# Two residual blocks in one kernel: where norms, moves, products, banks and relus of the Gram stages stand

## The chip, the cores and the metric

The kernel runs on one core of one Trainium2 chip, in fp32. The metric is device time in microseconds (us), the median of several runs. Engines are named as in the profile: PE (TensorE, matrix products), PEld (its weight loads), DVE (VectorE), ACT (ScalarE), POOL (GpSimd) and SP (the sync engine, which issues DMA transfers).

## The reference

Two bottleneck blocks follow each other, with weights of their own, on x of 64 x 1024 x 14 x 14. The batch norms use the statistics of the batch itself, so each needs the whole of the convolution ahead of it before its scale and shift are known.

```python
def block(x, w1, b1, g1, be1, w2, b2, g2, be2, w3, b3, g3, be3, residual_scale):
    out = relu(bn(conv(x, w1, b1, 1, 0), g1, be1))      # 1x1, 1024 -> 256
    out = relu(bn(conv(out, w2, b2, 1, 1), g2, be2))    # 3x3, 256 -> 256
    out = bn(conv(out, w3, b3, 1, 0), g3, be3)          # 1x1, 256 -> 1024
    out = softplus(residual_scale)[0] * out
    return relu(x + out)
# bn: mean and variance over (batch, height, width), eps 1e-5
```

## The kernel before, in words

All images' pixels (12,544) of the 256 middle channels stay on chip in one tile, `y_all`, as two slots of 128 channels. The work goes in stages, for each layer b = 0 and 1: conv1 (for layer 1 interleaved with layer 0's last convolution, in `fused`), conv2 (`conv2`, a Winograd form), the Gram stage (`gram` and `conv3_stats`), and the last convolution with the residual (`residual`, then `fused` for layer 0, `final` for layer 1).

**Why there is a Gram stage.** The third batch norm needs mean and variance of conv3's output, which isn't kept. They follow from the sums and the 256 x 256 matrix of products (the Gram matrix) of y after its norm, less a centre: the mean square of output channel o is w_o^T G w_o, and its mean comes from the sums. So `gram` makes G on TensorE, and `conv3_stats` multiplies it with w3.

**The begin of `gram` (L997 to L1176).** A product over pixels needs the pixels on the partitions, so y has to be transposed, 256 pixels at a time (`px`, one "pair" of column blocks). 49 pairs come out of the generator `pairs` (L1109). Two ways of transposing are used:

- `by_tensor` (L1081): four TensorE transposes into a PSUM bank, and a DVE add of the centre (L1093) into a tile `zt`. The first 8 pairs go this way; their pixels are the pieces `still`, of 4 pairs each.
- `by_vector` (L1099): DVE transposes 32 x 32 blocks (L1102) of a copy, `home(k)`, in which DMAs have already put the blocks in place (`move`, L1058, 16 DMAs for the first two pieces, 12 and four ACT copies, `stay`, for the others). These are the pieces `moved`: the first of 5 pairs, then six of 6 pairs. In layer 0 the second home is the tile `ws`, otherwise homes are x tiles.

Before a piece can be moved it is normed (`normed`, ACT, with relu, one instruction for each slot) and its centre is subtracted (`less`, DVE, L1044). The kept pieces are normed only. ACT, DVE and TensorE work of this stage is pinned to the order of the source (`tc.keep_in_program_order`), and each engine works its queue in that order; the order is written by hand, as conditions on the number n of the pair just yielded. DMAs of a `move` go to SP or POOL by their number, which is a list in L1064. TensorE takes the products of pair k after the transposes of pair k + 1: eight products into the two banks `upper` ("cp") and `lower` ("ap") for each of its two column blocks.

**The end: `conv3_stats` (L1178).** Only a part of the symmetric G is computed, with weights once or twice 1/12544 in `by`. DVE scales the banks into g0 and g1 (`scaled`, L1185), TensorE multiplies with w3 (for each half of the output channels: t0 and t1, the left and right halves of g0 and g1's columns, L1210), DVE multiplies by w3 again and adds (L1213, L1214), and TensorE sums over partitions by products with ones (into "ax" and "ap"). One conv3 product of image pair 0 (`made`) stands ahead of all that. `affine` then makes scale and shift in a chain of small DVE instructions.

**`residual` (L1225)** handles the first image pair: for each of 8 output groups a product (those in `made` exist already), a DVE add with scale (L1233), an ACT relu with shift (L1234), and one DMA for the whole. Which PSUM bank a product takes is by tag: the tags given, or for the others the cycle in `Psum`. In layer 0 only two products are in `made`; in layer 1 six.

**`fused` (L1270)** starts with 14 steps (`LAG`) of the last convolutions alone. A step is one product; what follows a product (`after1` and so on: a copy `cu` on ACT, a DVE add) is issued at the next step. The order of a unit is p1, p2, p6, p5, p7; p6 adds into the bank that `cu` copies after p1, and p7 into the one copied after p6.

Of the kernel before, what the change touches and what calls it, by code (L numbers as in the profile page):

```python
# [88 lines left out]
def bottlenecks(ctx: ExitStack, tc: tile.TileContext, x, w1s, w2s, w3s, pars, out):  # L89
# [907 lines left out]
    def gram(psum, pool, homes, aff, minus_c, beside):  # L997
# [60 lines left out]
        def move(k):  # L1058
            x, a, run = home(k)
            for i, j in itertools.product(range(4), range(4)):  # L1060
                if k > 1 and i == j:
                    continue
                n = 4 * i + j if k < 2 else 3 * i + j - (j > i)
                queue = nc.gpsimd if n in ((1, 3, 6, 8, 10, 13, 15) if k < 2 else (1, 3, 6, 8, 10)) else nc.sync  # L1064
                ins = queue.dma_start(  # L1065
                    out=x[32 * i : 32 * i + 32, :, j], in_=y_all[32 * j : 32 * j + 32, :, a + i * run : a + i * run + run]
                )
                tc.keep_in_program_order(ins)
# [40 lines left out]
        def pairs():  # L1109

            for a in 0, px:
                norm_vector(1, y_all[:, 1, a : a + px], aff)
                normed(a, a + px, (0,))
            center_row()
            normed(2 * px, 4 * px)
            rest = [(piece, s) for piece in still for s in range(MS)]
            for n, a in enumerate(a for piece in still for a in range(*piece, px)):
                yield by_tensor(a)
                if n == 0:
                    busy(psum, "ax", 1)  # L1120
                    normed(*moved[0])
                elif n == 1:
                    less(*moved[0])
                    move(0)
                    normed(*still[1])
                elif n == 3:
                    normed(*moved[1])
                elif n == 4:
                    less(*moved[1], both[:1])
                    normed(*moved[2])  # L1130
                elif n == 5:
                    less(*moved[1], both[1:])
                    move(1)
                elif n == 6:
                    less(*moved[2], both[:1])
                    normed(*moved[3])
            for k, (a, e) in enumerate(moved):
                for i in range((e - a) // px):
                    yield by_vector(k, i)
                    if k == 0 and i == 1:  # L1140
                        less(*moved[2], both[1:])
                        move(2)
                        stay(2)
                    elif i in (1, 3) and k and k + 2 < len(moved):
                        less(*moved[k + 2], both[i // 2 : i // 2 + 1])
                        if i == 3:
                            move(k + 2)
                            if k + 3 < len(moved):
                                normed(*moved[k + 3])
                            stay(k + 2)  # L1150
                    elif i in (0, 5) and k > 1 and rest:
                        piece, s = rest.pop(0)
                        less(*piece, (s,))
            assert not rest
# [23 lines left out]
    def conv3_stats(psum, one, grams, w3, mv, tags, spare):  # L1178
# [7 lines left out]

        scaled(g0[low], 0, upper[low], by[0][low])
        scaled(g0[high], Q + 1, upper[high], by[0][high])
        scaled(g1[low], 2 * Q + 1, lower[low, : 2 * Q + 1], by[1][low])
        n = Q + 1  # L1190
        for a, k in (1, 0), (3 * Q + 1, 1):
            scaled(g1[high], a, lower[high, k * n : k * n + n], by[1][high, k * n : k * n + n])
# [12 lines left out]
        for h in range(2):  # L1205
            cols = slice(h * half, (h + 1) * half)
            t0, t1 = (psum.tile(half * P, tag) for tag in tags[2 * h : 2 * h + 2])
            for i, g in enumerate((g0, g1)):
                for n, t in enumerate((t0, t1)):
                    matmul(t, g[:, 1 + n * P : 1 + n * P + P], w3[:, i, cols, :], start=i == 0, stop=i == 1)  # L1210
            qs = [q[:, s, h * half * P : (h + 1) * half * P] for s in range(MS)]
            for s, t in ((0, t0), (1, t1)):
                nc.vector.tensor_mul(qs[s], t, w3[:, s, cols, :].rearrange("p o c -> p (o c)"))  # L1213
            nc.vector.tensor_add(qs[0], qs[0], qs[1])  # L1214
# [10 lines left out]
    def residual(psum, xt, b, t, w3, aff, made=()):  # L1225
# [4 lines left out]
        for o in range(CS):  # L1230
# [3 lines left out]
            nc.scalar.activation(v, v, AF.Relu, bias=shift[:, o : o + 1])  # L1234

            step = CS if not tail else 1 if o + 2 >= CS else 2
            if (o + 1) % step == 0:
                queue = nc.gpsimd if step == CS else nc.scalar if o + 1 == CS else nc.sync
                queue.dma_start(
                    out=to[:, (o + 1 - step) * PX : (o + 1) * PX],  # L1240
                    in_=xt[:, o + 1 - step : o + 1, :].rearrange("p s f -> p (s f)"),
                )

# [26 lines left out]
    def fused(psum, pool, xpool, xs, w1, w3, aff, par, stats, one_done):  # L1270
# [18 lines left out]
        for i in range(LAG):  # L1289
            next(c)  # L1290
        while True:
# [164 lines left out]
    for b in range(2):  # L1456
# [7 lines left out]
        with tc.tile_pool(name=f"last_{b}", bufs=1) as one, tc.tile_pool(  # L1464
# [6 lines left out]
            with ExitStack() as scope:  # L1471
# [22 lines left out]
                if b == 1:  # L1494
                    made += [conv3(psum, 0, o, w3, tag) for o, tag in zip(range(2, 6), ("cy", "cp") * 2)]
# [4 lines left out]
                residual(psum, xs[0], b, 0, w3, aff, made)  # L1500
                weights = made_a + made_c
                with tc.tile_pool(name=f"rest_{b}", bufs=1) as pool:
# [5 lines left out]
                    fused(psum, pool, xpool, xs, *weights, aff, par[b + 1], stats1, one_done)  # L1508
# [40 lines left out]
```

## Time and profile before

| | us |
|---|---|
| median of 3 runs | 1932.78 (1932.09 to 1934.12) |
| the profiled execution, own time | 1934.62 |
| its span, first to last instruction | 1932.8 |
| PE busy, share of span | 1907.8, 99% |
| DVE busy | 1545.2, 80% |
| ACT busy | 1080.9, 56% |
| POOL busy | 563.8, 29% |
| Gram stage of layer 0, first to last `zt` product | 589.8 to 651.8 |
| Gram stage of layer 1, first to last `zt` product | 1550.0 to 1613.6 |

The profile is of one execution. "Busy" counts the time in which at least one instruction of an engine ran. A line of waits gives the waiting engine, the tile and source line of the waiting instruction, the one that released it, and then the sum, the number and the longest of these waits. A line of windows gives a stretch of time, the busy time of each engine with its number of instructions, the granted clock of TensorE as a share of full speed, the share of the DMA engines' time that was used, and GB/s. A line of the timeline gives start, duration, engine, source line, operation, written and read tiles, shape and count; a bracket at the end gives the idle time ahead of it and what ended it. A line of the chain gives start, duration and what the chain of work that ended last ran through.

### The profile page before, as it was taken

To read this page: it belongs to the slowest core of one execution; us is meant where nothing else is said; L and a number is where in the kernel's file an instruction comes from. 1 tells how busy PE (TensorE), PEld (TensorE's weight loads), DVE (VectorE), ACT (ScalarE), POOL (GpSimd) and SP (SyncE) were. 2 spreads that over 40 slices of the span, in tenths; PEclk is the share of its full clock that TensorE was granted. 3 is DMA by queue.
4 is the path that set the end of the run, shared out by engine and by line. 5 is a ranking of instruction groups with operands and counts; after the bars stand their busy time and mean duration, and the time that the engine had idled before them with its cause. 6 is when DMAs were issued, how large, how long until landed. Compare 5 with 4: busy or idle time off the path is not lost.

```text
span 1932.8 us, 28746 instructions
## 1 busy us (share of the span) xinstructions
PE 1907.8 (99%) x10246; PEld 1602.5 (83%) x10246; DVE 1545.2 (80%) x2481; ACT 1080.9 (56%) x2142; POOL 563.8 (29%) x680
## 2 busy tenths in 40 slices
PE   9999999999999999999999999999999999999999
PEld 5555557999997799999999999989999977555555
DVE  5778767999997767676776767689999986888886
ACT  2222214677777255555555555556777682666666
POOL 0111100211204133333433334302121041666664
PEclk9999999999999999999999999999999999999999
DMA  7777634787946534444444444258788466899998
GB/s 290 276 244 271 229 136 156 198 221 208 226 153 178 183 150 184 168 167 171 180 183 167 167 174 179 115 179 211 215 206 225 131 175 228 289 326 337 338 339 302
DMA packets 199071, 409.56 MB, mean 212 GB/s; under 512 B 37168, under 2 KB 175536, under 8 KB 182416
## 3 DMA queue, kind: packets, MB, share of 16 engines
q1 hardware_dynamic: 160128, 322.40, 48.4%
q0 software_dynamic: 33184, 34.25, 8.6%
q10 hardware_dynamic: 5616, 51.06, 6.3%
q8 instruction: 81, 1.33, 0.3%
q14 instruction: 62, 0.51, 0.1%
HBM read 263.75 MB, written 115.34 MB: 196 GB/s over the span
## 4 chain that ended last, share of the span: by engine, by line
PE 93%; DVE 3%; DMA 1%; ACT 1%; issue 1%; SPq 0%; POOL 0%; DVEq 0%; ACTq 0%; POOLq 0%
PE cy L171 17%; PE ay L171 17%; PE columns L171 13%; PE cp L171 12%; PE ap L171 10%; PE m L171 7%; PE l L171 6%; PE cx L171 5%; PE ax L171 4%; PE ps L171 1%; ACT y L334 0%; DMA home<-y 0%; DMA x<-mid 0%; SPq L1065 0%; DMA ws<-y 0%
## 5 line engine op out<-in xcount | busy, mean ns | idle before, releaser
L334 ACT ACTIVATE cu<-cy,scale 128x196 f32<-128x196 f32 (+1 forms) x552 | 256.8, 474 | 276.9 <-PE cy L171 271.7
L171 PE MATMUL columns<-v,ub 128*128 128x224 f32 (+1 forms) x1536 | 300.7, 337 | 0.0
L334 ACT ACTIVATE x<-x,shift 128x392 f32<-128x392 f32 x428 | 241.0, 613 | 59.6 <-POOL x L493 53.1
L171 PEld LDWEIGHTS columns<-v,ub 128*128 128x128 f32 x1536 | 269.2, 188 | 2.8
L467 DVE SCALAR_TENSOR_TENSOR x<-cp,scale,x 128x196 f32<-128x196 f32 (+1 forms) x368 | 178.0, 484 | 97.8 <-PE cp L171 96.5
L171 PE MATMUL cy<-ct,ws 128*128 128x196 f32 (+1 forms) x736 | 221.9, 383 | 1.8 <-ACT cu L334 1.7
L488 POOL TENSOR_TENSOR x<-x,cu 128x196 f32<-128x196 f32 (+1 forms) x184 | 159.7, 868 | 172.9 <-ACT cu L334 165.0
L171 PE MATMUL ay<-at,ws 128*128 128x196 f32 (+1 forms) x752 | 209.1, 381 | 0.0
L493 POOL TENSOR_TENSOR x<-x,cu 128x392 f32<-128x392 f32 x124 | 125.8, 1014 | 191.5 <-DVE x L467 191.5
L171 PEld LDWEIGHTS ay<-at,ws 128*128 128x128 f32 x752 | 136.5, 190 | 33.4
L171 PEld LDWEIGHTS cy<-ct,ws 128*128 128x128 f32 x736 | 133.4, 190 | 37.0 <-ACT cu L334 5.3
L171 PE MATMUL l<-diffs,ub 128*128 128x224 f32 (+1 forms) x768 | 149.1, 337 | 2.6 <-PE columns L171 2.6
L514 POOL TENSOR_TENSOR x<-x,cu 128x392 f32<-128x392 f32 x120 | 122.0, 1017 | 86.2 <-DVE x L467 71.8
L171 PE MATMUL m<-sums,ua 128*128 128x224 f32 (+1 forms) x752 | 145.9, 337 | 1.1 <-DVE sums L625 1.1
L334 ACT ACTIVATE au<-ay 128x196 f32<-128x196 f32 (+1 forms) x141 | 53.8, 381 | 156.9 <-PE ay L171 152.1
L171 PEld LDWEIGHTS l<-diffs,ub 128*128 128x128 f32 x768 | 134.3, 189 | 4.4 <-PE columns L171 3.9
L467 DVE SCALAR_TENSOR_TENSOR x<-cx,scale,x 128x196 f32<-128x196 f32 (+1 forms) x184 | 89.0, 484 | 57.0 <-PE cx L171 56.8
L171 PEld LDWEIGHTS m<-sums,ua 128*128 128x128 f32 x752 | 131.3, 189 | 2.9 <-DVE sums L625 2.5
L171 PE MATMUL cy<-y,w 128*128 128x196 f32 (+1 forms) x408 | 125.3, 393 | 0.0
L171 PE MATMUL cx<-y,w 128*128 128x196 f32 (+1 forms) x400 | 122.7, 391 | 0.0
L171 PE MATMUL cp<-y,ws 128*128 128x196 f32 (+1 forms) x368 | 113.6, 390 | 0.2 <-DVE x L467 0.2
L761 ACT ACTIVATE columns<-m 128x448 f32<-128x448 f32 (+1 forms) x160 | 78.5, 490 | 59.4 <-PE m L171 56.8
(219 smaller groups left out, 3973.1 us busy)
## 6 DMA issues: line engine op xcount, KB each, us to landing
x<-in_x SPq DMA_DIRECT2D x62, 1568.0 KB, 6.6
ub<-u SPq DMA_DIRECT2D x94, 768.0 KB, 5.3
x<-mid SPq DMA_DIRECT2D x32, 1568.0 KB, 7.8
mid<-x ACTq DMA_DIRECT2D x31, 1568.0 KB, 5.1
out<-x SPq DMA_DIRECT2D x123, 392.0 KB, 5.4
ua<-u SPq DMA_DIRECT2D x94, 256.0 KB, 3.0
u<-y POOLq DMA_DIRECT2D x48, 256.0 KB, 5.6
home<-y SPq DMA_DIRECT2D x72, 96.0 KB, 3.6
```

Source lines behind the costliest of these rows:

```text
L171: tc.keep_in_program_order(nc.tensor.matmul(*args, **kw))
L334: tc.keep_in_program_order(nc.scalar.activation(*args, **kw))
L467: nc.vector.scalar_tensor_tensor(v, bank, self.scale[:, o : o + 1], v, ALU.mult, ALU.add)
L488: nc.gpsimd.tensor_add(self.part(1, 1), self.part(1, 1), u3)
L493: nc.gpsimd.tensor_add(v, v, self.u12)
L514: nc.gpsimd.tensor_add(v, v, self.u12[:, i * self.n : (i + 1) * self.n])
L761: nc.scalar.activation(v, m, AF.Copy)
```

## The change

Both layers: of the begin of the Gram stage, DVE norms two more pieces of slot 1 that ACT normed (`norm_vector`, two DVE instructions: scale and shift, then the maximum with zero); some norms, `less` and moves take other places in the order; the moves of the first two pieces put 8 of 16 DMAs on POOL instead of 7. In `conv3_stats` the block of g1 that stood for the lower left is transposed on TensorE and put into g0, and each half has three products with w3 instead of four. Layer 0 only: three more conv3 products are issued ahead of `affine`, with other banks for these and for the rest; and the last two relus of `residual` and its store are handed to `fused`, which issues them after the third step of its begin.

```diff
@@ move
-                queue = nc.gpsimd if n in ((1, 3, 6, 8, 10, 13, 15) if k < 2 else (1, 3, 6, 8, 10)) else nc.sync
+                queue = nc.gpsimd if (n % 2 if k < 2 else n in (1, 3, 6, 8, 10)) else nc.sync
@@ pairs
             for a in 0, px:
                 norm_vector(1, y_all[:, 1, a : a + px], aff)
                 normed(a, a + px, (0,))
+            normed(2 * px, 4 * px, (0,))
             center_row()
-            normed(2 * px, 4 * px)
             rest = [(piece, s) for piece in still for s in range(MS)]
+            (second, end), half = still[1], sum(still[1]) // 2
             for n, a in enumerate(a for piece in still for a in range(*piece, px)):
                 yield by_tensor(a)
                 if n == 0:
                     busy(psum, "ax", 1)
+                    norm_vector(1, y_all[:, 1, 2 * px : 4 * px], aff)
                     normed(*moved[0])
                 elif n == 1:
                     less(*moved[0])
                     move(0)
-                    normed(*still[1])
+                    normed(second, end, (0,))
+                    normed(second, half, (1,))
                 elif n == 3:
+                    norm_vector(1, y_all[:, 1, half:end], aff)
                     normed(*moved[1])
                 elif n == 4:
-                    less(*moved[1], both[:1])
+                    less(*moved[1])
+                    move(1)
                     normed(*moved[2])
                 elif n == 5:
-                    less(*moved[1], both[1:])
-                    move(1)
+                    less(*moved[2], both[:1])
                 elif n == 6:
-                    less(*moved[2], both[:1])
+                    less(*moved[2], both[1:])
                     normed(*moved[3])
+                elif n == 7:
+                    move(2)
+                    stay(2)
             for k, (a, e) in enumerate(moved):
                 for i in range((e - a) // px):
                     yield by_vector(k, i)
-                    if k == 0 and i == 1:
-                        less(*moved[2], both[1:])
-                        move(2)
-                        stay(2)
-                    elif i in (1, 3) and k and k + 2 < len(moved):
+                    if i in (1, 3) and k and k + 2 < len(moved):
@@ conv3_stats
+        n = Q + 1
+        scaled(g1[high], 1, lower[high, :n], by[1][high, :n])
+        turned = psum.tile(P, "ax")
+        tc.keep_in_program_order(nc.tensor.transpose(turned, g1[:, 1 : P + 1], ident))
         scaled(g0[low], 0, upper[low], by[0][low])
         scaled(g0[high], Q + 1, upper[high], by[0][high])
+        nc.vector.tensor_copy(g0[low, 3 * Q + 1 : M + 1], turned[low, Q:])
         scaled(g1[low], 2 * Q + 1, lower[low, : 2 * Q + 1], by[1][low])
-        n = Q + 1
-        for a, k in (1, 0), (3 * Q + 1, 1):
-            scaled(g1[high], a, lower[high, k * n : k * n + n], by[1][high, k * n : k * n + n])
+        scaled(g1[high], 3 * Q + 1, lower[high, n : 2 * n], by[1][high, n : 2 * n])
...
-            for i, g in enumerate((g0, g1)):
-                for n, t in enumerate((t0, t1)):
-                    matmul(t, g[:, 1 + n * P : 1 + n * P + P], w3[:, i, cols, :], start=i == 0, stop=i == 1)
+            left, right = slice(1, P + 1), slice(P + 1, M + 1)
+            matmul(t0, g0[:, left], w3[:, 0, cols, :], start=True, stop=True)
+            matmul(t1, g0[:, right], w3[:, 0, cols, :], start=True, stop=False)
+            matmul(t1, g1[:, right], w3[:, 1, cols, :], start=False, stop=True)
@@ residual
-    def residual(psum, xt, b, t, w3, aff, made=()):
+    def residual(psum, xt, b, t, w3, aff, made=(), later=None):
...
-            nc.scalar.activation(v, v, AF.Relu, bias=shift[:, o : o + 1])
+            relu = partial(act, v, v, AF.Relu, bias=shift[:, o : o + 1])
+            if later is not None and o + 2 >= CS:
+                later.append(relu)
+            else:
+                relu()
...
-                queue.dma_start(
+                store = partial(
+                    queue.dma_start,
...
+                if later is not None:
+                    later.append(store)
+                else:
+                    store()
@@ fused
         for i in range(LAG):
             next(c)
+            if i == 2:
+                for run in begun:
+                    run()
@@ the two layers
-                if b == 1:
-                    made += [conv3(psum, 0, o, w3, tag) for o, tag in zip(range(2, 6), ("cy", "cp") * 2)]
+                tags = ("cy", "cp") * 2 if b else ("cy", "cx", "cy")
+                made += [conv3(psum, 0, 2 + i, w3, tag) for i, tag in enumerate(tags)]
+                if b == 0:
+                    psum.cycle = itertools.cycle(["ay", "ay", "cy"])
...
-                residual(psum, xs[0], b, 0, w3, aff, made)
+                later = None if b else []
+                residual(psum, xs[0], b, 0, w3, aff, made, later)
...
-                    fused(psum, pool, xpool, xs, *weights, aff, par[b + 1], stats1, one_done)
+                    fused(psum, pool, xpool, xs, *weights, aff, par[b + 1], stats1, one_done, later)
```

More of the change, by code (lines that the diff above doesn't have):

```diff
@@ L1268, in final, with fused @@
         residual(psum, xs[T - 1], 1, T - 1, a, aff)
-    def fused(psum, pool, xpool, xs, w1, w3, aff, par, stats, one_done):
+    def fused(psum, pool, xpool, xs, w1, w3, aff, par, stats, one_done, begun):
         def last_convs():
```

## The prediction

> **What bounds the kernel now.** I read the page first, then TensorE's waits, then the two Gram stages by windows, by the chain of waits and by the timeline. The page says who sets the time:
>
> ```profile
> PE 1907.8 (99%) x10246; PEld 1602.5 (83%) x10246; DVE 1545.2 (80%) x2481; ACT 1080.9 (56%) x2142; POOL 563.8 (29%) x680
> ```
>
> TensorE is the bound everywhere; time can only go where it idles, runs slowly, or has products fewer. Its waits over the whole span (total, times, longest in us):
>
> ```profile
> PE cp L171 <- DVE zt L1102: 5.7, 2, 2.9
> ...
> PE ay L171 <- DVE x L1233: 1.2, 1, 1.2
> ...
> PE cp L171 <- DVE zt L1093: 1.0, 2, 0.5
> ```
>
> Rows one and three are two waits in each Gram stage (layer 0 from 587 us, layer 1 from 1547 us); row two is layer 0's end. By windows (busy time by engine, then granted clock, DMA share, GB/s), first layer 0, then layer 1 on both sides of the long wait:
>
> ```profile
> 609.24:612.15 2.91, 0.00 (x2) 0.00 (x0) 0.76 (x2) 2.27 (x2) 0.00 (x0) 1.00 1.00 227
> ...
> 1569.47:1572.25 2.78, 0.01 (x2) 0.00 (x0) 0.76 (x2) 1.90 (x2) 0.00 (x0) 1.00 1.07 239
> 1572.25:1576.20 3.95, 3.95 (x34) 3.45 (x36) 3.95 (x6) 0.36 (x1) 0.10 (x1) 0.60 0.18 36
> ```
>
> TensorE stands for 2.9 and 2.8 us while the DMA engines are full, and in layer 1 it then runs 3.95 us at a clock of 0.60, which costs 0.40 x 3.95 = 1.6 us. What it waits for is the second moved piece; in SP's timeline of layer 0, and then in the chain:
>
> ```profile
> 593.38 6.71 SPq L1065 DMA_DIRECT2D home<-y  x9
> 600.19 6.38 SPq L1065 DMA_DIRECT2D ws<-y  x9
> 606.68 5.02 SPq L1065 DMA_DIRECT2D home<-y  x7
> ```
> ```profile
> 605.97 5.29 DMA ws<-y
> ```
>
> SP issues the second piece's 9 DMAs (0.71 us each) only once the first piece's 9 are out; the last, of 605.97, lands at 611.3. The end of layer 0's stage, in the chain and in TensorE's timeline:
>
> ```profile
> 653.37 0.86 PE cy L171 x2
> 654.23 0.86 PE cp L171 x2
> ...
> 659.38 0.86 PE cx L171 x2
> 660.24 1.73 PE ax L171 x16
> 661.97 1.80 PE ap L171 x16
> ```
> ```profile
> 667.60 1.55 PE L171 MATMUL ay<-y,w 128*128 128x392 f32 x4 [1.15 <-DVE x L1233]
> ...
> 676.11 0.60 PE L171 MATMUL cy<-ct,ws 128*128 128x196 f32 x2 [1.02 <-ACT cu L334]
> ```
>
> Eight products of 0.86 us stand on TensorE's path with no gap; then it waits 1.15 us for a bank, and 1.02 us for ScalarE's copy `cu`, which is queued behind the last relu (L1234, at 675.12).
>
> **What the Trainium skill says.** "TensorE: Matmul & The Clock Gate", Part 1 (the HAM clock gate): the array falls to half clock after an idle window of about 3.4 us that runs freely. The trace agrees in part: a wait of 2.78 us was followed by clock 0.60, one of 2.91 us was not, as a window that isn't tied to the work would give. "DMA: Bandwidth & Descriptors", Issuing engines are not separate DMA queues: all queues end on the same 16 engines, another issuer saves only issue time. The windows agree: DMA share 1.00 at 227 GB/s while SP and POOL both feed. "VectorE: DVE Perf Modes", The perf-mode tier table: fp32 `tensor_scalar` out of SBUF does two elements a cycle; L1044 agrees (0.89 us for 1280 elements, 1.00 for 1536, some 0.45 ns an element).
>
> **The change, part by part** (times of layer 0; layer 1's are 960.2 later).
>
> *Norms.* ScalarE loses two norms: slot 1 of 2px:4px and half of slot 1 of the last kept piece. It has 0.80 us for 512 columns, 1.23 for 1024. Its slot-0 norm of 2px:4px now stands ahead of `c_row`, in the 0.62 us in which ScalarE waited for it; `c_row`, and behind it the first `zt`, come 0.1 late, hidden by the second transposes (till 589.8). So the first moved piece's norms end at 592.45 - 1.5 + 0.1 = 591.05, the second piece's at about 598.0 - 1.4 - 0.4 = 596.2.
> VectorE gains two pairs of `tensor_scalar` on 512 columns. Rows: 0.41 and 0.29 us at 256. Unseen at 512: 0.96 at 0.5 ns an element, 1.2 at twice that; I take 1.05. The first pair (589.2 to 590.25) fills an 0.82 us gap and puts the second `zt` 0.3 late, for which nobody waits (its products start at 591.6). The `less` pair of piece 1 then ends at 592.6 instead of 593.36, and the third `zt` at 593.3 instead of 593.95. The 0.49 us wait goes: 0.45 a stage, bounds 0.15 and 0.5. **0.9**.
>
> *Second moved piece.* Its two `less` now stand together, before the sixth `zt`, and end at 598.05 instead of 599.47; that `zt` comes at 598.7, its products at 599.0: cover 0.3, so a slower `less` would show there. SP has 8 + 8 DMAs instead of 9 + 9: first piece 592.7 to 598.5, second 598.5 to 604.2, last issue near 603.5 instead of 605.97. POOL's eighth at 0.6 to 0.66 us makes it end at 602.9. With the landing of before (4 to 5.3 us) the piece is there at 607.5 to 608.8; a transpose (0.69) and 0.1 later TensorE can go on, 608.3 to 609.6. TensorE wants it 0.5 earlier than before, at 608.75. Left over 0 to 0.9, I take 0.5. If the piece is bound by DMA bandwidth, only the 0.8 us earlier start counts and 2.6 stay. So 2 x (2.85 - 0.5) = **4.7**, bounds 0.6 and 5.7. With an idle of 0.5 the clock stays up: **1.6**, bounds 0 and 1.6.
> The third piece moves forward with it: `less` one tensor step earlier, 12 DMAs (5 POOL, 7 SP) behind piece two on both queues, four ScalarE copies of 0.84. They'd be out by 609.3, landed by 614, wanted after piece two's six transposes, about 614. In the steady part VectorE stands at 5.00 of 5.00 us, so I give nothing there.
>
> *Six products.* Two of 0.86 go: 1.72 a stage. Added: a 128x128 transpose (0.15, from four in 0.59) after the first conv3 product, a 64-column copy on VectorE (0.2) that waits for it, with the remaining scalings and `by_mean` (0.75 + 1.28) queued behind, and the products into t1 waiting for all; t0's 0.86 covers the copy. VectorE's total from the last Gram product is 7.8 us plus some 1 of waits, against about 8.7 on TensorE before the `ap` sums: cover is gone, I charge 0.3. 2 x (1.72 - 0.15 - 0.3) = **2.5**, bounds 1.6 and 3.1.
>
> *Banks, layer 0.* Outputs 2 to 4 have cy, cx, cy, which are free, so TensorE runs four products (5.3 us) through the 3.1 us of scale and shift; outputs 5 to 7 take banks that are free by then. The 1.15 wait and 0.2 of refill go: **1.3**, bounds 0.9 and 1.4.
>
> *Relus later, layer 0.* `cu` no longer waits behind the last relu: the third product of the next convolution comes some 0.6 earlier. But both relus (0.62 each) now stand between the first and second `cu`, for which the fifth product waits: of the 0.6, 0.3 stays. **0.3**, bounds -0.5 and 0.7. The store on POOL delays nobody.
>
> Sum: 0.9 + 4.7 + 1.6 + 2.5 + 1.3 + 0.3 = 11.3. The profiled execution took 1934.62 (span 1932.8, and 1.8 around it): 1923.3. It lies 1.8 above the median of 1932.78, about one dip of the clock; if the median's runs had none, they gain only 9.7: 1923.1. I take **1923.0**.
>
> **The rivals.**
> A. *The moved piece is bound by bandwidth.* For it: share 1.00 at 604 to 612, and layer 1's last to land was a POOL transfer (8.83 us). Against: the DMA share is 0.25 at 590 to 595, so an earlier start has free engines. Then 2.6 us a stage and the dip stay: 0.9 + 0.6 + 2.5 + 1.3 + 0.3 = 5.6, about 1928.
> B. *VectorE becomes the bound at the ends.* The copy waits, `by_mean` and six multiplies of 0.69 follow in order. For it: VectorE's last add ended at 661.69, TensorE wanted it at 661.97. Then the ends give 0.6 instead of 2.5 and the later places 0.9: 11.3 - 2.6, about 1925.5.
> C. *Slower: the last stage turns from TensorE to DMA.* From 1634.84 to 1917.40 its 15 pairs take 18.84 us each, while the loads of x are issued every 19.2 (11 intervals from 1683.45 to 1895.01), some after 20.5, at 340 GB/s; at 1865 TensorE just waits, 0.23 us. If the stage were paced by loads, the loss passes the gain at 18.84 + 11.3 / 15 = 19.6 a pair; at 20 it is 17.4, so 1941. Against: loads and stores there are released by this stage's own work, so that it shifts as a whole, and no edit touches it.
>
> **How the numbers follow.** The forecast's own case (1920 to 1926) has 0.68, A 0.15, B 0.10, C 0.04, and 0.03 that the gains vanish where I don't see it. Upper bounds together give 13.5, off the median 1919.3; lower bounds together 2.9, 1929.9, but they'd need A and B at once, so I stop at A's upper half: range 1919.0 to 1928.5, which takes in B and leaves out C and a part of A. A measurement of this kernel can tell 0.2% (3.9 us) from no change, so faster begins below 1928.9: all of the first case, two thirds of A, most of B: 0.87; same 0.09; slower 0.04.
>
> **What would show it.** Right: TensorE's wait on `zt` L1102 under 1.3 us in each stage, none on L1093; no window at clock 0.60 after it; six rows of 0.86 between the first conv3 product and `ax`, 1.2 us less from the last Gram product to `ap`; no wait on `x` L1233, outputs 1 to 7 in 9.3 us. Wrong: waits over 2 us on L1102 (A), a wait of `ap` or `cp` on VectorE's copy or `home` (B), pairs of the last stage above 19.2 us (C), a `cu` wait longer than 1.02 before the fifth product.

## The result, and the profile after

The changed kernel takes 1928.03 us (median of 9 runs, 1926.99 to 1929.92) against 1932.78 us before (9 runs): ratio 0.9973, interval 0.9965 to 0.9982. (Here and below the ratio, with its 95% interval, is an estimate of its own and not the quotient of the two medians.) By the medians that is 4.75 us less, where 1923.0 was forecast; it lies 0.5 us inside the upper end of the forecast range (1928.5) and is rival A's number. The profiled execution took 1929.22 (span 1927.4), 5.4 less than the one before. In the page's line of engines TensorE has six instructions fewer (the four products that go are two instructions each, and two transposes come):

```profile
PE 1905.4 (99%) x10240; PEld 1600.4 (83%) x10240; DVE 1547.5 (80%) x2491; ACT 1077.5 (56%) x2140; POOL 568.5 (29%) x684
```

TensorE's waits over the whole span (total, times, longest):

```profile
PE cp L171 <- DVE zt L1102: 3.9, 3, 2.2
...
PE cy L171 <- ACT cu L334: 1.7, 4, 0.5
```

The rows for `zt` L1093 and for `x` L1233 are gone. The long wait on `zt` L1102 is not: 3.9 us in place of 5.7. The windows of the waits, layer 0 (with 3.6 us of work ahead), then layer 1's wait and what follows it (busy time by engine, clock, DMA share, GB/s):

```profile
605.50:610.39 4.89, 3.60 (x54) 3.17 (x50) 0.97 (x3) 3.02 (x2) 1.34 (x3) 1.00 1.08 233
1563.00:1567.16 4.16, 1.97 (x30) 1.56 (x26) 0.76 (x2) 2.08 (x2) 0.00 (x0) 1.00 1.06 247
1567.16:1572.20 5.04, 5.04 (x50) 4.48 (x52) 5.04 (x8) 1.42 (x2) 1.13 (x3) 0.66 0.20 41
```

The DMA engines are full while TensorE stands, as before, and layer 1 has its stretch at a low clock again. SP's timeline of layer 0 and the chain at the same place:

```profile
592.00 5.34 SPq L1065 DMA_DIRECT2D home<-y  x8
597.77 5.35 SPq L1065 DMA_DIRECT2D ws<-y  x8
603.23 16.04 SPq L1065 DMA_DIRECT2D home<-y  x13
```
```profile
599.90 5.04 DMA ws<-y
604.93 0.28 issue
605.22 4.43 DMA home<-y
609.65 0.70 DVE zt L1102
610.39 0.55 PE cp L171 x4
```

The second piece (`ws`) is issued as forecast, out by 603.1 on SP and by 603.6 on POOL. But its first transposed copy starts only at 609.6. The chain puts that down to a transfer of the third piece (`home`, issued at 605.22), which this copy doesn't read: that transfer updates a semaphore (a counter by which a transfer tells of its landing) that the second piece used too, and the profile takes the latest update for the release. What the line does show is that both pieces are on the engines together. The second piece's own last transfer lands at 608.96. After it VectorE works off six more wait instructions of this copy, each for two semaphores and 0.1 us apart (609.05 to 609.58), so that 0.67 us pass before the copy; in the kernel before, the transfer that landed last was the one waited for last, and 0.12 us passed. How long the second piece's transfers took, from issue to landing, stands under the tile `ws`, first for the kernel before, then after:

```profile
L1065 SPq DMA_DIRECT2D ws<-y x9: 586/602/1006, 600.2 to 606.0; - x9
...
DMA to landing us min/median/max: 2.8/3.4/5.3
```
```profile
L1065 SPq DMA_DIRECT2D ws<-y x8: 595/602/749, 597.8 to 602.5; - x8
...
DMA to landing us min/median/max: 4.4/5.1/6.1
```

Issued earlier and closer together, the transfers take longer in layer 0: a median of 5.1 us in place of 3.4. In layer 1 the median goes from 3.4 to 3.9. The end of layer 0's stage, in the chain and in TensorE's timeline:

```profile
652.00 0.11 PE ax L1193
652.10 0.86 PE cy L171 x2
652.97 1.94 PE cp L171 x4
654.90 0.86 PE cy L171 x2
655.76 1.72 PE cx L171 x4
657.48 1.73 PE ax L171 x16
659.21 1.79 PE ap L171 x16
```
```profile
671.20 0.60 PE L171 MATMUL cy<-ct,ws 128*128 128x196 f32 x2 [0.26 <-ACT cu L334]
...
672.53 0.60 PE L171 MATMUL cy<-ct,ws 128*128 128x196 f32 x2 [0.40 <-ACT cu L334]
```

Six products of 0.86 us, one of them with 0.2 of waiting inside its group (1.94 for two), then the sums without a gap. The third product of the next convolution waits 0.26 in place of 1.02.

Here is the span by stage, from milestones in the timeline (begin: first transpose of the stage to the last Gram product; end: from there to the last sum; residual: from there to the next stage's third matmul with x in layer 0, to its first with `ct` in layer 1):

| us | before | after | difference |
|---|---|---|---|
| up to layer 0's stage | 587.70 | 587.44 | -0.26 |
| layer 0: begin / end / residual | 64.16 / 11.90 / 18.61 | 63.04 / 10.52 / 16.88 | -1.12 / -1.38 / -1.73 |
| fused / conv2 | 582.25 / 283.31 | 582.27 / 283.85 | +0.02 / +0.54 |
| layer 1: begin / end / residual | 65.70 / 11.90 / 11.12 | 64.57 / 10.52 / 11.12 | -1.13 / -1.38 / 0 |
| last stage | 296.20 | 297.25 | +1.05 |

The ends give 4.5 us with layer 0's residual, the begins 2.2, the start 0.3, and 1.6 are lost in stages that the diff doesn't touch. This compares one profile with one; how far the begins repeat is seen below.

### The profile page after: what moved, and what is told of

It reads as the page before. It is cut to its first block, busy times and chain, and to the rows that moved or that the text cites. A ratio compares the mean times of both kernels' runs of the same rounds, so it can differ in the third digit from the quotient of the medians.

```text
span 1927.4 us, 28744 instructions
## 1 busy us (share of the span) xinstructions
PE 1905.4 (99%) x10240; PEld 1600.4 (83%) x10240; DVE 1547.5 (80%) x2491; ACT 1077.5 (56%) x2140; POOL 568.5 (29%) x684
## 4 chain that ended last, share of the span: by engine, by line
PE 92%; DVE 4%; DMA 2%; issue 1%; ACT 1%; POOL 0%; SPq 0%; DVEq 0%; ACTq 0%; POOLq 0%
PE ay L171 17%; PE cy L171 17%; PE columns L171 13%; PE cp L171 11%; PE ap L171 10%; PE m L171 7%; PE l L171 6%; PE cx L171 5%; PE ax L171 4%; PE ps L171 1%; DMA home<-y 1%; DMA x<-mid 0%; DMA out<-x 0%; DMA x<-in_x 0%; DVE v L631 0%
## 5 line engine op out<-in xcount | busy, mean ns | idle before, releaser
L334 ACT ACTIVATE x<-x,shift 128x392 f32<-128x392 f32 x452 | 255.0, 613 | 72.6 <-POOL x L493 53.5
L875 POOL DMA_DIRECT2D y<-f x24 | 30.8, 1521 | 275.1 <-DVE f L801 246.8
```

What stands on the lines that cost most here:

```text
L334: tc.keep_in_program_order(nc.scalar.activation(*args, **kw))
L875: nc.gpsimd.dma_start(out=out_rows[3][:, o], in_=fa[:, o, :full], accum_op=ALU.add)
```

## Experiments

Each of the twelve ran beside the kernel before, both on one chip; but the twelve used four chips (begin only to old list; changed kernel again to third later; third back to relus here; third after), so that between these groups only the ratios compare. "Wait" is TensorE's for the second moved piece, "copy" the start of VectorE's first transposed copy (L1102) of that piece, counted from the stage's first transpose; both for layer 0 / layer 1, from one profile each.

| run | median us, (before) | ratio, interval | wait us | copy us |
|---|---|---|---|---|
| the kernel before, first profile | 1932.78 | | 2.91 / 2.78 | 23.7 / 23.6 |
| the changed kernel, first profile | 1928.03 (1932.78) | 0.9973, 0.9965 to 0.9982 | 1.29 / 2.20 | 22.2 / 22.4 |
| begin only | 1933.82 (1935.21) | 0.9993, 0.9985 to 1.0001 | 1.71 / 1.50 | 22.5 / 21.7 |
| ends only | 1927.62 (1935.21) | 0.9968, 0.9955 to 0.9980 | 0.64 / 2.04 | 21.4 / 22.8 |
| filled wait | 1931.69 (1935.21) | 0.9985, 0.9977 to 0.9993 | 0 / 0 | 21.8 / 22.7 |
| old list | 1927.74 (1935.21) | 0.9963, 0.9950 to 0.9975 | 0.76 / 1.44 | 21.0 / 21.7 |
| changed kernel again | 1929.57 (1934.20) | 0.9975, 0.9964 to 0.9985 | 1.94 / 1.98 | 22.2 / 22.2 |
| old list again | 1927.69 (1934.20) | 0.9964, 0.9952 to 0.9977 | 2.58 / 1.56 | 22.8 / 21.8 |
| fewer bytes | 1923.25 (1934.20) | 0.9948, 0.9935 to 0.9960 | 0 / 0.97 | 20.2 / 21.2 |
| third later | 1929.32 (1934.20) | 0.9976, 0.9968 to 0.9984 | 1.45 / 2.40 | 22.5 / 22.6 |
| third back | 1928.02 (1934.74) | 0.9968, 0.9955 to 0.9980 | 1.51 / 2.38 | 21.7 / 22.6 |
| fewer bytes, old list | 1923.48 (1934.74) | 0.9942, 0.9928 to 0.9955 | 0 / 0.58 | 19.1 / 20.8 |
| relus here | 1928.27 (1934.74) | 0.9968, 0.9956 to 0.9981 | 1.32 / 1.92 | 21.5 / 22.1 |
| third after | 1936.77 (1934.78) | 1.0012, 1.0004 to 1.0020 | 0.78 / 1.19 | 21.0 / 21.4 |

In the texts that were written ahead of the runs, theory 1 is that the second moved piece is bound by the DMA engines, not by when it is issued. The main rival is that its landing is a latency after its last issue.

**The two halves of the change.** Begin only is the kernel before with the hunks of `move` and `pairs`; ends only is it with all the others:

```diff
+            normed(2 * px, 4 * px, (0,))
             center_row()
-            normed(2 * px, 4 * px)
...
-                queue = nc.gpsimd if n in ((1, 3, 6, 8, 10, 13, 15) if k < 2 else (1, 3, 6, 8, 10)) else nc.sync
+                queue = nc.gpsimd if (n % 2 if k < 2 else n in (1, 3, 6, 8, 10)) else nc.sync
```

> The kernel before with the change's begin of the Gram stage alone (norms, less, moves and queues), the ends as before. Theory 1 (the second moved piece is bound by the bandwidth of the DMA engines, so only its earlier start counts): each stage gains 1.1 us from its first transpose to its last product, as in the trace of the changed kernel, so about 1930.5 (ratio 0.9988); TensorE still waits 1.3 us (layer 0) and 2.2 us (layer 1) on the transposes of L1102, and the clock still drops after the wait of layer 1. Theory 2 (the prediction: SP's queue was the bound, and the begin loses its gain only together with the ends): waits under 1.0 us and no drop, 7.2 us less, 1925.6.

```diff
+        turned = psum.tile(P, "ax")
+        tc.keep_in_program_order(nc.tensor.transpose(turned, g1[:, 1 : P + 1], ident))
...
+                tags = ("cy", "cp") * 2 if b else ("cy", "cx", "cy")
```

> The kernel before with the change's ends alone (six products, the banks, the relus), the begin as before. Theory 1 (parts add up, ends worth what the trace of the changed kernel shows: 1.4 for each layer's products, 1.4 for the banks, 0.3 for the relus): 4.5 us less, 1928.3 (ratio 0.9977), so that the ends alone give nearly all of the whole change. Rival (the last stage, paced by its loads, takes back what layer 1's end gains): 3.1 us less, 1929.7, and a last stage over 1 us longer than in the kernel before.

By the ratios the begin alone gives 1.4 us (by its interval between 2.9 less and 0.2 more), which rules out the 7.2 of the prediction, and the ends alone 6.2 (3.9 to 8.7; 4.5 was expected). So the ends alone give as much as the whole change (0.9968 and 0.9973, with intervals that overlap): beside them the begin adds nothing that these runs can tell. The rival of ends only fell, its last stage is 0.3 us shorter than before. In the trace the ends give the same in every run that has them: 10.52 us from the last Gram product to the last sum (11.90 without), 16.88 of residual (18.61). The begin does not repeat. Ends only has the begin of the kernel before, and yet TensorE's waits for layer 0's second piece are short:

```profile
PE cp L171 <- DVE zt L1102: 0.6, 1, 0.6
PE cp L171 <- DVE zt L1093: 0.5, 1, 0.5
```

0.6 us, where the first profile had 2.9 with the same code. The first profile had caught a long wait. The length of layer 0's begin says the same: 64.2 and 61.9 us in the two profiles with the old code, 62.6 to 64.3 in six with the new one. In layer 1 a gain is left: 65.7 and 65.0 against 62.6 to 64.6.

**Filling the wait.** Dummy products on TensorE at the place of the wait keep it busy, against the low clock:

```diff
                     yield by_vector(k, i)
+                    if (k, i) == (1, 0):
+                        busy(psum, "ax", 4)
```

> The changed kernel with four 448-column dummy products into the free bank ax ahead of the second moved piece's first products (1.5 us of work in the wait). Theory 1 (the clock drops because TensorE stands still there): the window after the wait of layer 1 stays at clock 1.00 and 1.6 us are saved there; in layer 0, where the wait is 1.3 us, the fill costs 0.2 to 0.4: 1926.8 (ratio to the changed kernel 0.9994). Rival (the drop isn't tied to this wait, or comes anyway): clock 0.6 for 3 us again, and a time of 1928.0 to 1928.5.

I had mis-sized the filler: it takes 4.26 us of TensorE's timeline, with its own weight loads, not 1.5. So it costs more than the waits that it covers, both begins come to 64.81 us (63.04 and 64.57 in the first profile), and the time rises. No wait is left and the clock stays up in both layers; but it does so in four of the six profiles with the changed begin and no filler too, so this run doesn't show that the filler did it. A filler of this length buys nothing.

**The list of POOL's transfers.** The changed kernel with the list of before, twice, the second time beside the changed kernel on one chip:

```diff
-                queue = nc.gpsimd if (n % 2 if k < 2 else n in (1, 3, 6, 8, 10)) else nc.sync
+                queue = nc.gpsimd if n in ((1, 3, 6, 8, 10, 13, 15) if k < 2 else (1, 3, 6, 8, 10)) else nc.sync
```

> The changed kernel with the old list of queues (7 of 16 DMAs of the first two pieces on POOL, 9 on SP). Theory 1 (bandwidth): the second piece lands within 0.4 us of where it lands in the changed kernel, waits on L1102 1.3 and 2.2 us, time 1928.0 within 0.5. Theory 2 (SP's issues are the bound, as the prediction's step had it): one DMA more for each of two pieces on SP, 1.4 us later at 0.7 each, waits 2.7 and 3.6, 2.8 us more, 1930.8. Rival 3 (the even split makes both queues write the same 32 partitions at one time and slows them): the piece lands earlier than in the changed kernel, waits under 1 us, 1926.

> The changed kernel once more, so that the next three stand beside it on one chip. If the landing of the second moved piece scatters from execution to execution, its wait (1.29 us in layer 0 and 2.20 us in layer 1 in the first profile) moves by up to 1 us with the same issue times; if it is fixed by the issue times, both waits come back within 0.2 us. The ends of both Gram stages should come back to 0.02 us (10.52 us from the last Gram product to the ap sums' end). Time some 4.5 us under the kernel before on the same chip.

> The changed kernel with the list of before for POOL's DMAs of the first two pieces (7 of 16 in place of every second one). Theory 1, all transfers end on the same engines and the list only shifts who issues: the second piece's wait stays within 0.5 us of the changed kernel's and the time within 0.5 us of it. Rival, every second DMA in POOL's queue makes blocks of the same target rows collide or be issued late: the wait in layer 0 is again under 0.9 us, none at 16 us into the stage, and the time is 1 to 3 us under the changed kernel's on this chip.

The first run seemed to speak for the old list (waits 0.76 and 1.44); the second had 2.58 and 1.56. So the list alone doesn't set the wait. Nor does the time of SP's issues: with the old list the last one comes 0.2 to 1.4 us later than the changed kernel's last issue (15.8 to 17.0 us into the stage, against 15.6), and the copies come no later (21.8 in the mean of four, against 22.2). The theory that SP's issues are the bound had expected waits of 2.7 and 3.6. The changed kernel's own waits came back as 1.94 and 1.98, after 1.29 and 2.20 with issue times of the second piece that agree within 0.4 us: the wait scatters by itself. On the one chip the old list's median is 1.9 us lower, but the intervals overlap. Where it differs in the traces is elsewhere: conv2 and the last stage (below).

**Fewer bytes.** Four of the second piece's 16 blocks lie on the diagonal and need no move between partitions; ScalarE copies them, as it does for the later pieces:

```diff
-                if k > 1 and i == j:
+                if k and i == j:
                     continue
-                n = 4 * i + j if k < 2 else 3 * i + j - (j > i)
-                queue = nc.gpsimd if (n % 2 if k < 2 else n in (1, 3, 6, 8, 10)) else nc.sync
+                n = 3 * i + j - (j > i) if k else 4 * i + j
+                queue = nc.gpsimd if (n in (1, 3, 6, 8, 10) if k else n % 2) else nc.sync
@@ pairs, n == 4
                     normed(*moved[2])
+                    stay(1)
```

> The changed kernel with the four diagonal blocks of the second moved piece copied by ScalarE in place of DMAs: 12 of 16 transfers are left, a quarter of its bytes goes. Theory 1, bound by the DMA engines: a quarter of about 1.3 MB at 0.21 MB per us is 1.5 us, so the wait of 1.3 to 2.2 us falls to 0 to 0.7 and the time by 1.5 to 3 us. Rival, the landing is a latency after the last issue that has nothing to do with bytes: the last issue comes two DMAs (1.4 us) earlier and the result is the same, but then the piece lands the same 7 us after its last issue, while under theory 1 it lands 4 to 6 us after it. ScalarE's four copies of some 0.84 us may delay the next norms: then the wait moves to the third piece.

> The second piece's four diagonal blocks by ScalarE, as in the run with fewer bytes, and the first piece with POOL's list of before (7 of 16). Theory 1 expects the second piece's wait at 0 to 1 us in both layers, as there. If the list matters for the first piece, its products start without a wait and nothing else changes: within 1 us of the run with fewer bytes (10 to 11 us under the kernel before). If the phase of SP's queue is what made the last stage 1.1 us longer in the runs with every second transfer on POOL, the last stage stays at 295.9 to 296.3 here.

The second of these has, beside that, `n in (1, 3, 6, 8, 10, 13, 15)` for the first piece. In its trace the tile `ws` reads:

```profile
L1065 SPq DMA_DIRECT2D ws<-y x7: 586/602/789, 599.1 to 603.3; - x7
...
L334 ACT ACTIVATE ws<-y x4: 826/842/845, 599.5 to 602.0; 32x768 f32<-32x768 f32 x4
...
DMA to landing us min/median/max: 3.0/3.4/4.3
```

The last issue, at 603.3, is 15.1 us into the stage, where the changed kernel's is at 15.6; but the copy starts at 19.1 in place of 22.2. Over both runs and layers the copies come 1.9 us earlier (20.3 in the mean, against 22.2 in the changed kernel's two profiles), for a last issue that is 0.9 earlier in the mean (14.2 to 15.1 into the stage, against 15.6). The two layers differ. In layer 0 the piece lands 3.8 and 4.9 us after its last issue, against about 5.9 in both of the changed kernel's profiles: there fewer bytes land sooner, as theory 1 says. In layer 1 it lands 5.9 and 6.3 us after it, against 5.7 and 5.8: what is gained there is the earlier issue and a shorter row of waits on VectorE, as the rival says. So the run speaks for theory 1 in layer 0 alone. TensorE's waits of the second run are short enough that no stretch at a low clock follows:

```profile
PE cp L171 <- DVE zt L1102: 1.4, 2, 0.8
```

The four copies (0.84 us each) bring no new wait: the 0.8 us one, in layer 1 some 52 us into the stage, stands in the changed kernel's second profile too. These two are the fastest kernels of the study: 0.9942 (0.9928 to 0.9955) and 0.9948, against 0.9973 and 0.9975 of the changed kernel, and gain more than the 1.5 to 3 us that were expected: by the medians on one chip the first is 6.3 us under the changed kernel. Of the 5.1 us between their two profiles 4.6 are in the begins, and in layer 0 that is the wait of 1.94 and the stretch at a low clock behind it. The two don't differ measurably from each other. The last stage of the second took 296.5 us, a little over the 295.9 to 296.3 that I expected.

**The third piece out of the way.** Three attempts to send the third piece's 12 transfers later. The first puts `move(2)` and `stay(2)` behind the last block of the first moved piece, the second puts the second half of `less(*moved[2])` and both back to where they were before the change, behind the second block, and the last puts all three behind the first transposed copy of the second piece:

```diff
-                elif n == 7:
-                    move(2)
-                    stay(2)
...
+                    if (k, i) == (1, 0):
+                        less(*moved[2], both[1:])
+                        move(2)
+                        stay(2)
```

> The changed kernel with the third piece's transfers and ScalarE's four copies issued some 6 us later, in the middle of the first piece's products. Theory 1, bound by the DMA engines, which the third piece's 12 transfers enter before the second has landed: the second piece lands 1 us or more earlier (wait 0 to 1 us in both layers), while the third is late by up to 2 us, seen as a wait at its own products. Rival, transfers are served in the order of issue and the third piece's don't disturb the second's: the second's wait stays at 1.3 to 2.2 us.

> The changed kernel with the second half of the third piece's subtractions, its 12 transfers and ScalarE's four copies back where the kernel before had them, after the second block of the first moved piece; unlike the run before, the transfers now wait for a subtraction that VectorE does later. From the windows the DMA engines are full from 8.5 to 24 us into the stage; pieces one, two and three are some 4.2 MB, at 0.22 MB per us 19 us. Theory 1, the DMA engines' bandwidth is shared by all that is issued: with the third piece's 1.1 MB out of the way the second lands 1 to 2 us earlier, its first transposed copy starts 20 to 21 us into the stage (22.2 to 22.6 in three runs of the changed kernel) and the wait is 0 to 0.8 us; the third piece may then be waited for. Rival, transfers are served in order of issue: the second's copy stays at 22.2 to 22.6 and the wait at 1.3 to 2.4 us.

> In both runs meant to take the third piece out of the way, its transfers were issued at 15.8 to 16.6 us into the stage as before, since VectorE runs ahead: they tell nothing. Here the second half of its subtractions comes after VectorE's first transposed copy of the second piece, which itself waits for that piece: no transfer of the third can be under way before the second has landed. Theory 1, the bandwidth is shared by all that is issued: the second piece's first transposed copy starts 19.5 to 21 us into the stage in place of 22.2 to 22.6, and its wait is under 0.8 us; the third piece, issued from some 21 us on, is waited for by 2 to 5 us instead. Rival, transfers are served in order of issue, or the landing is a latency of its own: the copy stays at 22.2 to 22.6 us, the wait at 1.3 to 2.4 us, and the third's wait comes on top. The time is worse than the changed kernel's in both, by 2 to 8 us; the copy's start decides.

The first two failed as experiments. VectorE and the queues run ahead of TensorE, so that SP issued the third piece's first transfer 15.8 to 16.6 us into the stage, as in the changed kernel (15.8). They only add samples: copies at 21.7 to 22.6. The third did move them, to 22.6 and 23.1. Its windows in layer 0:

```profile
600.00:604.00 4.00, 4.00 (x56) 3.38 (x54) 3.08 (x6) 2.46 (x2) 3.61 (x7) 1.00 0.98 221
604.00:608.00 4.00, 4.00 (x62) 3.62 (x60) 1.07 (x2) 0.00 (x0) 0.00 (x0) 1.00 0.93 182
608.00:612.00 4.00, 3.02 (x42) 2.32 (x39) 3.06 (x4) 1.40 (x2) 1.15 (x2) 1.00 0.05 10
```

After 608 almost nothing moves, where the changed kernel's DMA engines were full to 610; the second piece starts to be copied at 608.94, 21.0 us into the stage, and in layer 1 at 21.4. That is earlier than every run with the changed kernel's move of this piece (21.5 to 22.7 in layer 0 or 1 of seven runs), by 1.0 us against their mean of 22.2. The landing itself, at 20.7 and 20.8, is earlier than all fourteen of theirs (21.05 to 21.82) and 0.7 us ahead of their mean; the rest is VectorE's row of waits. So the third piece's transfers do delay the second's, as far as two stages can show it; one stage with the old list had its copy at 21.0 with the third piece in the way. I had expected 19.5 to 21 and a wait under 0.8; it was 0.78 and 1.19. Without the third piece the landing is inside what the prediction had said (607.5 to 608.8, which is 19.8 to 21.1 into the stage of before), with the engines at 0.93 by the second piece alone. The third is then waited for by 1.95 and 3.87 us, and the whole is slower than before.

**Relus at their old place.** The changed kernel with the last two relus and the store issued in `residual`:

```diff
-                later = None if b else []
+                later = None
```

> The changed kernel with layer 0's last two relus and the store back at their old place, ahead of the next stage's first copies on ScalarE; banks and six products as changed. My sum: later relus are worth 0.3 us, so from the end of the ap sums to the third product with x it is 17.2 us in place of 16.88, the third product waits again for cu (0.26 us with the relus later, 1.02 before), the fifth hardly. Rival, with the new banks TensorE is ahead and ScalarE would be late by the whole of both relus: 1.2 us. The other rival, below nothing: the relus later only move the wait from the third to the fifth product, the difference is under 0.1 us. The time itself can't tell 0.3 us; the trace can.

Residual takes 17.33 us in place of 16.88. The two waits on `cu`:

```profile
671.82 0.60 PE L171 MATMUL cy<-ct,ws 128*128 128x196 f32 x2 [1.12 <-ACT cu L334]
...
672.93 0.60 PE L171 MATMUL cy<-ct,ws 128*128 128x196 f32 x2 [0.18 <-ACT cu L334]
```

The third product waits 1.12 and the fifth 0.18, where it is 0.26 and 0.40 with the relus later: of 0.86 gained 0.22 are given back at the fifth, and more at the waits behind it. The later relus are worth 0.45 by the residual's length, forecast 0.3; the time can't show it. Neither rival (1.2, or under 0.1) holds.

## Why the prediction was right in sign and range and wrong in its middle

**What failed: "Second moved piece", 4.7 us, the step "With the landing of before (4 to 5.3 us)" and what follows it.** The issue moved as worked out (SP out at 603.1, the last issue forecast near 603.5). Then the gain was lost on the way to TensorE. These are the second piece's last issue, its last landing and the start of its first copy, in us into the stage, as means over the traces:

| begin of the stage | traces | layer 0: issue, landing, copy | layer 1: issue, landing, copy |
|---|---|---|---|
| before (first profile, ends only) | 2 | 18.0, 22.4, 22.6 | 17.0, 23.0, 23.2 |
| changed, with its list | 7 | 15.6, 21.5, 22.0 | 15.5, 21.4, 22.3 |
| changed, old list | 2 | 16.7, 21.8, 21.9 | 15.8, 21.5, 21.7 |
| fewer bytes, both lists | 2 | 15.0, 19.4, 19.7 | 14.3, 20.4, 21.0 |
| third after | 1 | 15.7, 20.7, 21.0 | 15.1, 20.8, 21.4 |

Over both layers the last issue comes 2.0 us earlier, the landing 1.3 and the copy 0.7, where the step has the landing 2.5 to 3.8 earlier and the copy with it. *The landing:* in layer 0 it follows the last issue by 5.9 us in place of 4.5, because the same 16 transfers, behind the first piece's, come to engines that are full, and the third piece, which the change moves forward too, comes right behind them. The text said of the third piece "I give nothing there"; that was considered for VectorE and TensorE, not for the DMA engines. In layer 1 the landing did move with the issue; but there it followed the last issue by 6.2 us in the first profile already, and "4 to 5.3" was layer 0's alone. (That transfer was SP's; the 8.83 us that the prediction gives to a POOL transfer in layer 1 are a chain line of two transfers, the later one of the third piece.) *The copy:* the step puts nothing between landing and copy. It took 0.1 to 0.2 us before, and 0.3 to 1.0 with the changed list, mostly for VectorE's row of waits (in layer 1 up to 0.4 of it comes after the row and stays unexplained): with the old list SP's last transfer, which lands last, stands last or next to last in it, with the new list the last to land stands further ahead. TensorE wants the piece 0.5 us earlier as forecast, so that of the wait's reduction 0.3 us a stage is left: 2.1 in the mean before (four stages), 1.8 after (twelve, without the filler).

The argument against rival A, that the share was 0.25 at 590 to 595, was beside the point: what counts is the share from 596 on, when the pieces are under way. "DMA: Bandwidth & Descriptors", Issuing engines are not separate DMA queues, in the Trainium skill says that transfers of all issuers interleave on the same 16 engines; that was quoted, and not applied to the third piece. Third after shows it in both layers, fewer bytes in layer 0.

**A sample was taken for a constant.** The 2.9 and 2.8 us from which the step starts were long ones: the same begin gave 0.64 and 2.04 in ends only, and the mean of these four stages is 2.1. So some 0.7 us a stage was counted as gain that the profile had only by chance: with the rest of the step right, 1.6 us a stage were to be won (2.1 less 0.5), not 2.35.

**Clock, 1.6: not had in the profile.** The stretch at low clock is still in both of the changed kernel's profiles. Over all profiles it may be rarer: it follows this wait in two of four stages with the old begin, and in two of twelve with the changed one. In the traces it lasts 3.41 us at half speed, 1.7 us lost (twice that after the 3.87 us wait of third after). It followed waits for moved pieces of 1.94, 1.95 and 2.58 in layer 0 and of 2.04, 2.20 and 2.78 in layer 1, but not others of 1.92, 1.98, 2.38, 2.40 and 2.91, and none that was shorter. Layer 0 of the changed kernel's second profile shows the shortest, the wait and the stretch behind it:

```profile
609.46:611.40 1.94, 0.02 (x2) 0.00 (x0) 0.74 (x2) 0.14 (x1) 0.00 (x0) 1.00 1.09 246
611.40:616.00 4.60, 4.58 (x42) 4.01 (x44) 4.60 (x7) 0.96 (x2) 0.70 (x2) 0.63 0.41 92
```

That is what a window of 3.4 us that isn't tied to the work would do ("TensorE: Matmul & The Clock Gate", Part 1, in the Trainium skill), except that a wait of 1.94 us doesn't fill such a window; the measurement decides. No wait under 1.9 us was followed by it, so the 0.5 of the working would have been safe in these traces; the changed kernel's waits were 1.29 to 2.20.

**Norms, 0.9: right as to the place.** The wait on `zt` L1093 is gone in both layers; one of 0.45 at the first moved piece stands in layer 0 in its stead in some runs (0.45, 0.35 and 0.61, in three of the seven). A pair of `tensor_scalar` at 512 columns took 0.97 us, forecast 1.05.

**Six products, 2.5: 2.76 measured** (2 x 1.38), inside the bounds. The cover for VectorE's copy costs about 0.2 a stage, 0.3 was charged. **Banks, 1.3, and relus, 0.3: 1.73 together** measured, of which 0.45 by the relus as undone, so by the difference 1.3 by the banks, which no run changed alone. Rival B fell: the `ap` sums follow the `ax` sums with no gap.

**Rival C fell, but its "no edit touches it" was too strong.** In the changed kernel's last stage TensorE waits for x (rows of waits from 1650 us on):

```profile
PE cp L171 <- DVE x L467: 0.7, 2, 0.6
```

In the seven traces with the changed kernel's list in both layers and its ends, the last stage took 296.9 to 297.3 us and conv2 283.7 to 283.9; in the two with the old list and all else changed, 295.9, and 283.3 or 283.4. That is 1.5 us in the mean, in stages that no edit touches, and most of the 1.9 between the two medians on one chip. The list leaves a different number of transfers on SP, so that later transfers use other semaphores and waits for them stand in another order; whether that is the cause was not tried, and begin only (299.2 in the last stage) fits no simple rule. It stays open.

Summed up: 4.5 by the ends, against 4.1 forecast; 2.2 by the begins in the profile, and 1.4 in begin only with an interval that takes in nothing, against 7.2; 1.6 lost in the other stages of that profile, against none. The mechanism of the likeliest case failed at the begins. Rival A's happened there in the main: by the prediction's own signs layer 1's wait of 2.20 us and the low clock behind it speak for A, while layer 0's 1.29 is just under the 1.3 that it had set. That the time is A's number is partly luck: A had 1.5 at the begins and 4.1 at the ends and no loss elsewhere. And that the time lies in the range is owed to the part that was kept for A and B, not to the case that was given 0.68.

## What to carry to other kernels

Before you issue a transfer earlier, sum the bytes of all that is under way between its issue and its need, and divide by the rate that the windows show: where the DMA engines are already full, much of an earlier issue can go into a longer transfer (here 1.5 of 2.4 us in layer 0, nothing in layer 1), and moving fewer bytes (here by four copies on ScalarE) made the fastest kernel. Look also at what stands between the last landing and the work that waits for it: many small transfers mean many waits. A wait at the end of a shared resource scatters from run to run; take its length from several executions before you count its removal as a gain. To send work later, tie it to something that really happens later: a place further down in the source does nothing if the queues run ahead.

## What the hardware showed unasked

Blocks of 32 partitions between tiles on chip moved at some 180 to 260 GB/s when the DMA engines were full (shares of 0.9 to 1.1), not at the 340 GB/s that the loads and stores of the last stage reached. The same transfers, the last of them issued within 0.5 us, landed up to 0.8 us apart in different executions (21.05 to 21.82 us into the stage), and their first copy started up to 1.1 us apart. An instruction that needs the landings of 16 transfers stood behind a row of wait instructions, two semaphores each and 0.1 us apart: with the last landing early in the row, 0.3 to 1.0 us passed before it started, with the last landing at its end 0.1 to 0.2. And half clock followed waits of 1.94 and 1.95 us.
